# Moving the first batch's token loads and first products to later places in a two-layer kernel, and some consumers in its scans a step or two later

## The chip, the cores and the metric

The kernel is one program on one core of a Trainium2 chip. The core has five engines that each work through their own queue in order: TensorE (PE), VectorE (DVE), ScalarE (ACT), GpSimd (POOL) and SyncE (SP, which only issues transfers here; POOL issues transfers too). The metric is the device time of one execution in microseconds (us).

## The reference, cut to what matters

Eight batches of 512 tokens of 256 values go through two layers. In layer 0 a token-by-token recurrence runs over the 512 tokens (16 heads with 16x16 states), then each token goes through one of eight experts. Layer 1 is ordinary causal attention with 16 heads and a softmax, then a dense mixture of eight small experts.

```python
h = _layernorm(x) * (1 + ca) + sa
x = x + ga * _L0_attn_ref(h, ...)        # recurrence: M += beta * k (v - M k)
h = _layernorm(x) * (1 + cb) + sb
x = x + gb * _L0_ffn_ref(h, ...)         # top-1 of 8 experts, 256 -> 1024 -> 256
h = _layernorm(x) * (1 + ca) + sa
x = x + ga * _L1_attn_ref(h, ...)        # q, k, v products, softmax attention
h = _layernorm(x) * (1 + cb) + sb
x = x + gb * _L1_ffn_ref(h, ...)         # weighted sum over 8 dense experts
```

## The kernel before

All data is float32. The 512 tokens of every batch are cut into four token tiles of 128 (tile i = 0 to 3). For layer 0 all eight batches of one token tile are worked on together.

**The scans.** `scan(i)` is the recurrence over the 128 tokens of tile i, for all 128 pairs of batch and head at once. One step is four DVE instructions in a chain: L640 (state times key), L644 (sum), L650 (outer product), L655 (state minus update). While scan i runs, other work is queued between its steps: the preparation of tile i+1 (`front(i + 1)`) and the attention output, routing and part of the experts of tile i-1 (`follow(i - 1)`). Each such piece has a number, the scan step after which it is due. `run` calls the pieces in the order of these numbers, and `tc.issue_after(step)` holds a piece's instructions on DVE behind the DVE instruction that ends the step. Instructions on other engines get no such edge: their place follows from the order of the text and from when the tile scheduler, which fixes each engine's queue at build time, takes them to be ready.

**`front(i, at)`** works per pair of batches p and batch b = 2p + c. `stats(p)` loads tokens (SP) and makes mean and deviation on ACT (its last instruction is the square root, L501). `normal(p)` is two small DVE instructions (L517, L518). `turn(b)` normalizes and transposes (ACT L140 and L145, PE L143), `project(b)` makes the q, k, v and beta products (PE L535, L539; ACT L543 to L549). `squares(b)` sums q*q and k*k on DVE (L553). `roots` and `scales` (ACT L565, L566; DVE L570; POOL L588) follow for each half of the batches, and `heads` at `at + 46` and `at + 49` lays out K and V for the next scan. `at` is 30 for tile 1 and 47 for tiles 2 and 3.

**`attend(i)`**, in its end: `roots` (DVE L824, behind ACT L809), `rest(b)` adds the attention output to the tokens (ACT L828, POOL L831 and L832 for tiles 0 to 2, then a store), and `stats(b)` takes their statistics on DVE (L840, L841).

**The slot tiles.** `route(i)` sorts the 1024 tokens of a token tile by expert into 15 slot tiles of 128 rows and scatters them to `hs_d` (POOL L1023, eight indirect transfers). `experts(i)` then walks over the slot tiles j = 0 to 14. `turn(j)` loads the rows (SP L1061, tile `hslot`, two buffers) and transposes them (PE L1064, ACT L1068). The first half of a slot tile is 32 matmuls (L1083) with weights w0, the second half 16 matmuls (L1102) with weights w1. `fetch(j, part)` gathers an expert's weights, 1 MB for w0 and as much for w1 (POOL L1044, two buffers each). The result takes a bias on POOL (`ysb`, L1108) and is stored to `ys_d` (POOL L1109). The order in the text is: fetch (0,0), (0,1), (1,0), then for each j the first half, fetch (j+1, 1), rows of j+1, second half, bias and store, fetch (j+2, 0).

When all 15 slot tiles of a token tile are stored, each batch's 128 results are gathered back (POOL L1117), multiplied by a gate (POOL L1153) and added to the tokens in memory by an accumulating transfer (POOL L1154, `x<-yrow`). For token tile 2 the gathered tile is `yrow`, from a tag with two buffers.

**The last stretch of layer 0.** For the last token tile, `x_last` takes a buffer of that same tag `yrow`. It is loaded at the start of `experts(3)`, ahead of `turn(0)` on SP:

```python
if i == NT - 1:
    x_last = fp.tile([P, D], F32, tag="yrow", name="x_last", bufs=2)
    nc.sync.dma_start(x_last, x2d[0][i])
```

The loads of the first batch's other three token tiles (`xs_first`, SP L1113) stand in the text at j = 7. The beginning of layer 1 for the first batch (`prologue`, 14 pieces: `norm`, five staged pieces of normalizing, transposing and v products, `both(0)` and `both(1)` with the q and k products of three token tiles at L261, then the same for the last token tile) is merged into the list of `experts(3)`, whose halves stand at 10j and 10j + 3, by

```python
last.append((102 + 4 * k if k < NT + 4 else 201 + k, piece))
```

so that `both(0)` stands at 126 and `both(1)` at 130, between the halves of slot tiles 12 and 13. `place1` loads layer 1's expert weights (`ew`, SP L212, two transfers of 1 MB) just ahead of `experts(3)`. After the last slot tile comes the return of the first batch's last token tile (`rows`, POOL L1117, DVE L1128 and L1129 with `x_last`), then the last prologue pieces, and the first scores of layer 1 (PE L1304).

Of the kernel before, what the change touches and what calls it, by code (L numbers as in the profile page):

```python
# [11 lines left out]
F32 = mybir.dt.float32  # L12
# [7 lines left out]
P = 128  # L20
B = 8
S = 512
D = 256
# [40 lines left out]
def tile_two_layers(ctx: ExitStack, tc: tile.TileContext, t: dict, out: bass.AP):  # L64
# [217 lines left out]
    with ExitStack() as l0:  # L282
# [166 lines left out]
        def front(i, at):  # L449
# [102 lines left out]
            def squares(b):  # L552
                nc.vector.tensor_reduce(  # L553
                    ss[:, :, b, :], got["sq", b].rearrange("p s (n d) -> p s n d", d=HD),
                    AX.X, ALU.add,
                )
# [51 lines left out]
            for p in range(B // 2):  # L608
                if i > 0:
                    pieces.append((at + 8 * p, lambda p=p: stats(p)))  # L610
                    pieces.append((at + 8 * p + 4, lambda p=p: normal(p)))
                elif p == 0:
                    pieces.append((at, stats_first))
                for c in range(2):
                    b = 2 * p + c
                    pieces.append((at + 8 * p + 3 * c + 4, lambda b=b: turn(b)))

                    late = 4.5 if i == 0 else 0
                    pieces.append((at + 8 * p + 3 * c + 4 + late, lambda b=b: project(b)))
                    pieces.append((at + 8 * p + 3 * c + 11, lambda b=b: squares(b)))  # L620
            for h in range(B // n):
                last = at + 16 * h + (23 if i else 39)
                pieces.append((last, lambda h=h: roots(h)))
                pieces.append((last + 2, lambda h=h: scales(h)))
            pieces.append((at + 46, lambda: heads("K", qk[:, 1], 1.0)))
# [31 lines left out]
        def attend(i, qk, V, x1, norms):  # L657
# [198 lines left out]
            for h in range(2):  # L856
                pieces.append((16 * h + 25, lambda h=h: roots(h)))
                for b in range(4 * h, 4 * h + 4):
                    pieces.append((13 * h + 25 + b, lambda b=b: rest(b)))
                    pieces.append((12 * h + 29 + b, lambda b=b: stats(b)))  # L860
            return got, pieces


# [167 lines left out]
        def experts(i, slot, idx):  # L1031


            if i == NT - 1:
                x_last = fp.tile([P, D], F32, tag="yrow", name="x_last", bufs=2)
                nc.sync.dma_start(x_last, x2d[0][i])
            ws = {}

            def fetch(j, part):
                if j >= NSLOT:  # L1040
                    return
                first, n = (0, WONE) if part == 0 else (WONE, WROW - WONE)
                w = fp.tile([P, n], F32, tag=f"w{part}", name=f"w{part}_{i}_{j}", bufs=2)
                issued["fetch"] = nc.gpsimd.indirect_dma_start(  # L1044
                    out=w,
                    out_offset=None,
                    in_=t[f"wrows{part}"],
                    in_offset=bass.IndirectOffsetOnAxis(ap=idx[:, j : j + 1], axis=0),
                    bounds_check=NE * P - 1,
                    oob_is_err=False,  # L1050
                ).ins
                ws[j, part] = w

            turned = {}

            def turn(j):

                if j >= NSLOT:
                    return
                hr = fp.tile([P, D], F32, tag="hslot", name=f"hslot{i}_{j}", bufs=2)  # L1060
                issued["rows"] = nc.sync.dma_start(hr, hs_d[i][j * P : (j + 1) * P, :]).ins  # L1061
                pt = bank()
                for c in range(2):
                    nc.tensor.transpose(  # L1064
                        pt[:, c * P : (c + 1) * P], hr[:, c * P : (c + 1) * P], ident
                    )
                hT = fp.tile([P, 2, P], F32, tag="hTs", name=f"hTs{i}_{j}", bufs=2)
                nc.scalar.copy(hT, pt[:, :D].rearrange("p (c t) -> p c t", c=2))  # L1068
                turned[j] = hT

            for j, part in ((0, 0), (0, 1), (1, 0)):
                fetch(j, part)
            turn(0)
            for j in range(NSLOT):
                hT = turned.pop(j)
                act = fp.tile([P, NFC, P], F32, tag="act", name=f"act{i}_{j}")
                w = ws[j, 0]
                for half in range(2):
                    ph = bank()
                    for q in range(4):  # L1080
                        f = half * 4 + q
                        for k in range(2):
                            nc.tensor.matmul(  # L1083
                                ph[:, q * P : (q + 1) * P],
                                w[:, k * FF + f * P : k * FF + (f + 1) * P],
                                hT[:, k, :],
                                start=(k == 0),
                                stop=(k == 1),
                            )
                    for q in range(4):  # L1090
                        f = half * 4 + q
                        nc.scalar.activation(  # L1092
                            act[:, f, :], ph[:, q * P : (q + 1) * P], AF.Relu,
                            bias=w[:, 2 * FF + f : 2 * FF + f + 1],
                        )
                fetch(j + 1, 1)
                yield
                turn(j + 1)
                w = ws[j, 1]
                py = bank()  # L1100
                for f in range(NFC):
                    nc.tensor.matmul(  # L1102
                        py[:, :D], act[:, f, :], w[:, f * D : (f + 1) * D],
                        start=(f == 0), stop=(f == NFC - 1),
                    )
                ysb = fp.tile([P, D], F32, tag="ysb", name=f"ysb{i}_{j}", bufs=2)
                nc.scalar.copy(ysb, py[:, :D])
                nc.gpsimd.tensor_add(ysb, ysb, w[:, NFC * D :])  # L1108
                nc.gpsimd.dma_start(ys_d[i][j * P : (j + 1) * P, :], ysb)  # L1109
                fetch(j + 2, 0)  # L1110
                if i == NT - 1 and j == NSLOT // 2:
                    for k in range(i):
                        nc.sync.dma_start(w1["xs"][:, k, :], x2d[0][k])  # L1113
                yield

            def gather(b, dst):
                nc.gpsimd.indirect_dma_start(  # L1117
                    out=dst,
                    out_offset=None,
                    in_=ys_d[i],  # L1120
                    in_offset=bass.IndirectOffsetOnAxis(ap=slot[:, b : b + 1], axis=0),
                )

            if i == NT - 1:
                rows = [w1["rows"][:, b * D : (b + 1) * D] for b in range(B)]
                for b in range(B):
                    gather(b, rows[b])
                nc.vector.tensor_mul(rows[0], rows[0], gates[1][:, 0, :])  # L1128
                nc.vector.tensor_add(w1["xs"][:, i, :], rows[0], x_last)  # L1129
                yield  # L1130
                with tc.issue_after(w1["ready"]):
                    for b in range(1, B):
                        nc.vector.tensor_mul(rows[b], rows[b], gates[1][:, b, :])
                        nc.gpsimd.dma_start(x2d[b][i], rows[b], accum_op=ALU.add)
                yield
                return

            if i < NT - 2 and "fetched" not in w1:
                fetched = ap.tile([P, P, HD], F32, tag="K", name="fetched")
                w1["fetched"] = fetched.rearrange("p t d -> p (t d)")  # L1140
            queue = []
            for b in range(B + DEPTH[i]):
                if b < B:
                    if i < NT - 2:
                        yr = w1["fetched"][:, b * D : (b + 1) * D]
                    else:
                        yr = fp.tile([P, D], F32, tag="yrow", name=f"yrow{i}_{b}", bufs=2)
                    with tc.issue_after(issued["scatter" if i == NT - 2 else "fetch"]):
                        gather(b, yr)
                    queue.append(yr)  # L1150
                if b >= DEPTH[i]:
                    yr, k = queue.pop(0), b - DEPTH[i]
                    nc.gpsimd.tensor_mul(yr, yr, gates[1][:, k, :])  # L1153
                    nc.gpsimd.dma_start(x2d[k][i], yr, accum_op=ALU.add)  # L1154
                yield
# [123 lines left out]
        begun = list(prologue(0, first, w1["xs"], (tuple(range(NT - 1)), (NT - 1,))))  # L1279

        for k, piece in enumerate(begun):
            last.append((102 + 4 * k if k < NT + 4 else 201 + k, piece))
        run(last)

    rec.close()
# [345 lines left out]
```

## Time and profile before

| | us |
|---|---|
| median of 3 runs | 2255.97 (2253.57 to 2258.22) |
| the profiled execution's own time | 2256.92 |
| its span in the profile | 2255.2 |
| scans and what runs beside them, some 65 to 1107 | 1042 |
| attention of token tile 3, its routing, slot tiles of token tile 2 to the last, 1110 to 1211 | 101 |
| from the last matmul of token tile 2's slot tiles to the first of token tile 3's, 1211 to 1264 | 53 |
| the 15 slot tiles of token tile 3, 1264 to 1385 | 121 |
| return of the first batch's last tokens, to the first scores, 1385 to 1402 | 17 |
| layer 1, 1402 to 2255 | 853 |

The median is 0.95 us below the profiled execution's own time, and 1.7 us of that time lie around the span. Lines of the profile are read thus: a start in us from the beginning of the span, a duration in us, the engine, the line of the kernel (L1083 is line 1083), the operation, "out<-in" by the names of the program's tiles, shapes, and a count. What stands in brackets is how long the engine sat idle before and who ended that. "SPq" and "POOLq" are the queues that issue transfers.

### The profile page before, as it was taken

Reading aid. Unit: us, or ns where it says so; the run is one execution under the profiler, and the core shown is the slowest. Engines: PE = TensorE matmul, PEld = TensorE weight load, DVE = VectorE, ACT = ScalarE, POOL = GpSimd, SP = SyncE. Lnnn points to the kernel's source line nnn. Section 1 sums busy time; section 2 is a strip of 40 time slices with the busy share of each in tenths; the row PEclk is TensorE's granted clock in tenths of the full one; section 3 lists DMA queues with packets and bytes.
Section 4 is the critical chain, followed back from the end, with each engine's and each line's share of the span. In section 5 each row is a group of like instructions: output and inputs, shape, how many; then the busy total and the mean of one; then the engine's idle time right before and its main releaser. Section 6 shows DMA issues by size and latency. Waiting matters only on the chain.

```text
span 2255.2 us, 32318 instructions
## 1 busy us (share of the span) xinstructions
PE 1726.5 (77%) x10874; PEld 1195.3 (53%) x10874; DVE 1595.2 (71%) x4533; ACT 1076.8 (48%) x2672; POOL 589.8 (26%) x791
## 2 busy tenths in 40 slices
PE   5334027479696887939893597999999999999997
PEld 3212025359574785738762596565555555555553
DVE  3899999899987999899652002686675767666654
ACT  5144025465356643613341244877475665747431
POOL 1102014145253453624374443010201011010111
PEclk9566567599798998959996798899999999999998
DMA  5110000178002680138665582000101010100001
GB/s 161 48 45 10 0 1 11 34 263 312 32 13 86 251 309 31 46 143 300 178 112 172 178 315 61 13 12 12 23 14 22 15 29 11 24 12 13 17 17 17
DMA packets 88630, 189.57 MB, mean 84 GB/s; under 512 B 13689, under 2 KB 67105, under 8 KB 75665
## 3 DMA queue, kind: packets, MB, share of 16 engines
q0 software_dynamic: 33696, 137.43, 19.0%
q1 hardware_dynamic: 54768, 50.09, 7.9%
q8 instruction: 86, 1.41, 0.3%
q14 instruction: 80, 0.65, 0.1%
HBM read 175.10 MB, written 36.93 MB: 94 GB/s over the span
## 4 chain that ended last, share of the span: by engine, by line
PE 42%; DVE 26%; issue 14%; ACT 7%; DMA 6%; POOL 5%; SPq 0%; POOLq 0%; ACTq 0%; DVEq 0%
PE ps L1469 6%; DVE state L644 6%; PE ps L1083 5%; PE ps L1330 5%; DVE state L655 5%; DVE terms L640 5%; DVE upd L650 5%; PE ps L1102 4%; PE ps L1304 3%; PE ps L535 3%; PE ps L1351 2%; DMA w<-in_wrows,idx 2%; PE ps L261 2%; DVE sc L1313 1%; PE ps L244 1%
## 5 line engine op out<-in xcount | busy, mean ns | idle before, releaser
L1318 ACT ACTIVATE pr<-sc,low 128x384 f32<-128x384 f32 (+3 forms) x512 | 255.6, 556 | 196.7 <-DVE low L1313 194.5
L1313 DVE CUSTOM_DVE_ANT_0 sc<-ps,strips 128x384 f32<-128x384 f32 (+3 forms) x512 | 225.4, 485 | 87.4 <-PE ps L1304 56.6
L1083 PE MATMUL ps<-hTs,w 128*128 128x128 f32 x1920 | 236.8, 284 | 19.9 <-DMA w<-in_wrows,idx 13.5
L1083 PEld LDWEIGHTS ps<-hTs,w 128*128 128x128 f32 x1920 | 233.3, 200 | 27.2 <-issue 13.1
L644 DVE TENSOR_REDUCE state<-terms 128x16 f32<-128x272 f32 x512 | 227.2, 444 | 15.8
L655 DVE TENSOR_TENSOR state<-state,upd 128x256 f32<-128x256 f32 x511 | 223.1, 437 | 14.8
L1469 PE MATMUL ps<-ew,hTd 128*128 128x512 f32 x512 | 232.9, 608 | 0.0
L640 DVE TENSOR_TENSOR terms<-state,K 128x256 f32<-128x256 f32 x512 | 216.0, 422 | 14.4
L1102 PE MATMUL ps<-w,act 128*128 128x256 f32 x960 | 220.8, 384 | 6.1 <-DVE dm L820 6.1
L650 DVE TENSOR_TENSOR upd<-K,state 128x256 f32<-128x256 f32 x511 | 214.2, 419 | 15.6
L1092 ACT ACTIVATE act<-ps,w 128x128 f32<-128x128 f32 x480 | 137.1, 371 | 152.8 <-PE ps L1083 151.7
L1330 PE MATMUL ps<-cst,pr 128*128 128x128 f32 x1280 | 192.4, 296 | 14.9 <-DVE low L1313 12.5
L1102 PEld LDWEIGHTS ps<-w,act 128*128 128x128 f32 x960 | 180.0, 193 | 29.5 <-DVE dm L820 6.6
L1474 DVE SCALAR_TENSOR_TENSOR accd<-ps,wtd,accd 128x256 f32<-128x256 f32 x256 | 123.8, 483 | 99.8 <-PE ps L1469 87.7
L1330 PEld LDWEIGHTS ps<-cst,pr 128*128 128x128 f32 x1280 | 149.8, 149 | 83.7 <-DVE low L1313 24.2
L1469 PEld LDWEIGHTS ps<-ew,hTd 128*128 128x128 f32 x512 | 96.4, 193 | 121.2 <-issue 107.6
L1478 POOL TENSOR_TENSOR accd<-accd,bc_g 128x256 f32<-128x256 f32 x28 | 20.4, 728 | 528.5 <-DVE accd L1474 528.5
L1044 POOL DMA_INDIRECT w<-in_wrows,idx x120 | 123.2, 1027 | 127.8 <-ACT hTs L1068 55.9
L1304 PE MATMUL ps<-kT,qTc 32*128 32x128 f32 (+3 forms) x1024 | 132.2, 491 | 5.4 <-DVE low L1313 3.8
L1339 DVE COPY prT<-ps 128x512 f32<-128x512 f32 (+3 forms) x256 | 117.0, 484 | 10.4 <-PE ps L1330 10.0
L674 PE MATMUL ps<-cst,V 128*128 128x128 f32 x64 | 12.5, 378 | 124.2 <-DVE V L646 124.2
L1337 ACT COPY prT<-ps 128x512 f32<-128x512 f32 (+3 forms) x256 | 98.9, 414 | 8.6 <-PE ps L1330 8.2
(264 smaller groups left out, 2939.4 us busy)
## 6 DMA issues: line engine op xcount, KB each, us to landing
hs<-zero SPq DMA_DIRECT2D x4, 1920.0 KB
hslot<-hs SPq DMA_DIRECT2D x60, 128.0 KB
ys<-ysb POOLq DMA_DIRECT2D x60, 128.0 KB, 3.8
x<-in_x SPq DMA_DIRECT2D x32, 128.0 KB
strips<-strip_d SPq DMA_DIRECT2D x16, 256.0 KB
out<-accd POOLq DMA_DIRECT2D x32, 128.0 KB, 3.1
wm<-in_wmod SPq DMA_DIRECT2D x4, 768.0 KB
xt<-in_x SPq DMA_DIRECT2D x12, 256.0 KB
```

Source lines behind the costliest of these rows:

```text
L640: nc.vector.tensor_mul(term[:, :, :HD], M, K[:, s, :].unsqueeze(1).to_broadcast([P, HD, HD]))
L644: nc.vector.tensor_reduce(delta, term, AX.X, ALU.add)
L650: nc.vector.tensor_mul(upd, K[:, s, :].unsqueeze(2).to_broadcast([P, HD, HD]), delta.unsqueeze(1).to_broadcast([P, HD, HD]),)
L655: yield nc.vector.tensor_sub(M, M, upd).ins
L1083: nc.tensor.matmul(ph[:, q * P : (q + 1) * P], w[:, k * FF + f * P : k * FF + (f + 1) * P], hT[:, k, :], start=(k == 0), stop=(k == 1),)
L1092: nc.scalar.activation(act[:, f, :], ph[:, q * P : (q + 1) * P], AF.Relu, bias=w[:, 2 * FF + f : 2 * FF + f + 1],)
L1102: nc.tensor.matmul(py[:, :D], act[:, f, :], w[:, f * D : (f + 1) * D], start=(f == 0), stop=(f == NFC - 1),)
L1304: made = nc.tensor.matmul(pscs[r][:, :W], qT[rows, g, o, i * P : (i + 1) * P], kT[rows, g, :W], start=True, stop=True,)
L1313: nc.vector.tensor_tensor_reduce(out=sc[:, :W], in0=pscs[r][:, :W], in1=strips[:, n, S - W :], scale=1.0, scalar=3.0e38, op0=ALU.add, op1= ...
L1318: nc.scalar.activation(pr, sc[:, :W], AF.Exp, bias=low, scale=-1.0)
L1330: nc.tensor.transpose(pt[:, (i - j) * P : (i - j + 1) * P], prs[r, i][:, j * P : (j + 1) * P], ident,)
L1469: nc.tensor.matmul(pe, hT[0][:, k, cols], ew[:, k, e : e + 2, :], start=(k == 0), stop=(k == 1),)
```

## The change

In `front`, for token tiles 1 to 3: `normal` goes from `at + 8p + 4` to `at + 8p + 5`; `turn` and `project` go one step later, `squares`, `roots` and `scales` two steps later; `heads` stays. In `attend`, `stats` goes one step later for all token tiles. In `experts(3)`, the load of `x_last` leaves the start and stands with the three loads of `xs_first` at j = 7, all four held on SP behind the load of the ninth slot tile's rows. In the list of the last stretch, `both(0)` and `both(1)` of the first three token tiles go from 126 and 130 to 151 and 152, behind the second half of the last slot tile at 143. No instruction is added or removed.

```diff
@@ front
                 if i > 0:
                     pieces.append((at + 8 * p, lambda p=p: stats(p)))
-                    pieces.append((at + 8 * p + 4, lambda p=p: normal(p)))
+                    pieces.append((at + 8 * p + 5, lambda p=p: normal(p)))
                 elif p == 0:
                     pieces.append((at, stats_first))
                 for c in range(2):
                     b = 2 * p + c
-                    pieces.append((at + 8 * p + 3 * c + 4, lambda b=b: turn(b)))
-
-                    late = 4.5 if i == 0 else 0
+                    pieces.append((at + 8 * p + 3 * c + (5 if i else 4), lambda b=b: turn(b)))
+
+                    late = 4.5 if i == 0 else 1
                     pieces.append((at + 8 * p + 3 * c + 4 + late, lambda b=b: project(b)))
-                    pieces.append((at + 8 * p + 3 * c + 11, lambda b=b: squares(b)))
+                    pieces.append((at + 8 * p + 3 * c + (13 if i else 11), lambda b=b: squares(b)))
             for h in range(B // n):
-                last = at + 16 * h + (23 if i else 39)
+                last = at + 16 * h + (25 if i else 39)
@@ attend
-                    pieces.append((12 * h + 29 + b, lambda b=b: stats(b)))
+                    pieces.append((12 * h + 30 + b, lambda b=b: stats(b)))
@@ experts
-            if i == NT - 1:
-                x_last = fp.tile([P, D], F32, tag="yrow", name="x_last", bufs=2)
-                nc.sync.dma_start(x_last, x2d[0][i])
...
                 if i == NT - 1 and j == NSLOT // 2:
-                    for k in range(i):
-                        nc.sync.dma_start(w1["xs"][:, k, :], x2d[0][k])
+                    x_last = fp.tile([P, D], F32, tag="yrow", name="x_last", bufs=2)
+                    with tc.issue_after(issued["rows"]):
+                        nc.sync.dma_start(x_last, x2d[0][i])
+                        for k in range(i):
+                            nc.sync.dma_start(w1["xs"][:, k, :], x2d[0][k])
@@ the last stretch
         for k, piece in enumerate(begun):
-            last.append((102 + 4 * k if k < NT + 4 else 201 + k, piece))
+            place = 102 + 4 * k if k < NT + 2 else 145 + k if k < NT + 4 else 201 + k
+            last.append((place, piece))
```

## The prediction, made before the result was known

> **What bounds the kernel now.** I read the busy time by stage first, then the chain of waits through the last stretch of layer 0, then the queues of POOL and PE there, and last the waits of DVE during the scans. The stages (columns: window, length, busy us of PE, PEld, DVE, ACT, POOL, granted clock, DMA share, GB/s):
>
> ```profile
> 890.00:1110.00 220.00, 170.89 (x1281) 150.83 (x1279) 198.05 (x506) 85.62 (x266) 97.83 (x133) 0.88 0.49 165
> 1211.00:1264.00 53.00, 0.29 (x2) 0.00 (x0) 4.25 (x6) 0.37 (x1) 30.43 (x34) 0.55 0.64 186
> 1264.00:1385.00 121.00, 119.48 (x784) 109.53 (x784) 3.21 (x11) 51.64 (x166) 44.99 (x54) 0.98 0.60 217
> 1385.00:1402.00 17.00, 6.26 (x30) 5.30 (x34) 4.64 (x14) 4.08 (x12) 11.83 (x14) 0.60 0.33 78
> ```
>
> In the scans DVE is the pace (198 of 220). Then 53 us follow in which PE does nothing, then 121 in which PE is never idle, then a hole of 17. The chain of waits names the end of the 53:
>
> ```profile
> 1257.20 3.16 DMA x<-yrow
> 1260.49 0.34 SPq L1036
> 1260.87 3.10 DMA hslot<-hs
> 1264.10 0.67 PE ps L1064 x2
> ```
>
> L1036 is `x_last`. It needs a `yrow` buffer, and gets one when the seventh accumulating transfer of token tile 2 has landed. The rows of slot tile 0 (`hslot`) stand behind it on SP. SP's own waits give 42.2 us to L1036. The scatter that makes these rows had been over since about 1217, when `ew`, which also waits for it, was issued. So 42 us are an accident of a shared buffer tag. What would stop PE next, if the rows came early, is seen in POOL's timeline (start, duration, line, idle time before and who ended it):
>
> ```profile
> 1219.53 1.04 POOL L1044 DMA_INDIRECT w<-in_wrows,idx  x1 [0.30 <-issue]
> ...
> 1230.07 1.01 POOL L1044 DMA_INDIRECT w<-in_wrows,idx  x1 [0.30 <-issue]
> ...
> 1259.23 0.93 POOL L1154 DMA_DIRECT2D x<-yrow  x1 [0.30 <-POOL yrow L1153]
> 1271.75 1.09 POOL L1044 DMA_INDIRECT w<-in_wrows,idx  x1 [11.59 <-ACT hTs L1068]
> ```
>
> Four weight fetches are out by 1231: both halves of slot tiles 0 and 1. The fifth, tile 2's w0, is the next instruction on POOL after the last accumulate of token tile 2.
>
> **`x_last` and `xs_first`, behind the ninth rows.** SP issues `ew` at 1217.09 in 1.11 us, so `hslot` 0 can go out at 1218.2. It lands 3.1 us later as it did alone (1221.3), or at the latest when the traffic of `ew` ends: the DMA share stays at 0.8 or more until 1238. From landing to the first matmul took 1.1 us, and two slot tiles take 15.8 (1265.22 to 1281.05). So tiles 0 and 1 are done between 1238 and 1255, and PE then waits for tile 2's w0. POOL's queue is built before the run, and the change touches no line of POOL there, so I take the order of the trace: all eight gathers, then the fetch. It issues at 1259.23 + 0.93 + 0.30 = 1260.5 and lands 6.8 us later (median of the 22 fetches from 1270 to 1350): 1267.3. Before, tile 2 began at 1281.05. The clock is half again after that wait: the first half took 5.07 us after the 52.8 us hole against 3.73 in the next tile. With a cold tile's 8.58 us (1265.22 to 1273.80), tile 3 starts at 1275.8 instead of 1288.29: **12.5 us gained**. The other fetches keep up: tile 2's w1 issues at 1263.8 and lands at 1270.6, before its second half at 1272.4; tile 3's w0 lands at 1271.9. Ends of this term: 4.5, if the fetch takes the 14.8 us of the longest weight wait in the chain (at 1100.5), and some 36, if POOL's order lets fetches in between (a rival below).
>
> The four moved loads cost SP some 1.7 us (0.34 + 1.38) in the middle of tile 8, behind rows that are already out; the next rows are not needed for most of a tile, so nothing on the path. They add 0.5 MB to the transfers there. A fetch was issued at 1278.99 for a tile that began at 1288.29, 9.3 us later, and takes 6.8: 2.5 us of cover. The statistics and normalizing of these tokens, done at 1265 before, now fall into tiles 8 to 11 on a nearly idle DVE (3 of 121 us) and on ACT (52 of 121): nothing, or up to 1.2 us if two of ACT's 0.6 us pieces get ahead of a tile's activations.
>
> A rule speaks against splitting the tiles by a new hole. The Trainium skill, "TensorE: Matmul & The Clock Gate", section "Why this matters for your kernels", wants no PE gap over some 3 us, since one idle window brings half clock, and Part 1 puts the warming at about 3.4 us. By it a second cold start costs 1.7 us (half of 3.4, an estimate from that page), and the total would be 0.4 us smaller. The rows say 5.07 - 3.73 = 1.34, which the 12.5 contains.
>
> **`both(0)` and `both(1)`, behind the last slot tile.** PE was the pace (119.5 of 121), and these stood in its path:
>
> ```profile
> 1365.00 2.74 PE L261 MATMUL ps<-hTc,wqkv 128*128 128x384 f32 x8
> 1371.15 2.75 PE L261 MATMUL ps<-hTc,wqkv 128*128 128x384 f32 x8
> 1380.98 3.62 PE L1102 MATMUL ps<-w,act 128*128 128x256 f32 x16
> 1394.71 0.69 PE L179 MATMUL ps<-cst,xnc 128*128 128x128 f32 x2 [10.12 <-ACT xnc L172]
> ```
>
> The chain counts 2.58 us for each: 5.2 us leave the tile path. They enter a hole of 10.1 us that waits for bias, store and gather. Their ACT work (1.23 + 0.58, twice, some 1.4 us behind PE) ends about 7 us into the hole; ACT's next due instruction came at 1393.34, 8.8 us in. So **5.2 us gained**, with the hole's remaining 5 us as cover; without cover it would be 0. The clock had fallen by 1388, 3.4 us after the last matmul, and a hole of 4.9 still lets it fall: no gain there (if it held, up to 3 us, from 0.69 to 0.38 and the like).
>
> **The scans.** DVE's waits from 60 to 990:
>
> ```profile
> DVE stf L840 <- POOL x L832: 8.5, 8, 1.4
> DVE ss L553 <- ACT sq L549: 6.9, 5, 3.5
> DVE ms L824 <- ACT ms L809: 4.6, 3, 2.7
> DVE rsa L517 <- ACT sda L501: 3.8, 5, 0.9
> ```
>
> A step is 1.87 us (four instructions), and a wait of DVE moves everything behind it. `stats` (L840): the waits sit in scans 2 and 3, 0.94, 0.99, 1.40, 0.91 each. One step more between POOL and DVE can give one step at most, for POOL does one batch in about 2.6 us and stays the slower: **1.87 us in each of two scans, 3.7**. `squares` (L553): 2.53 and 3.49 are the first of scans 1 and 2, due exactly at their place (after 59 steps), so two steps (3.7 us) clear them. But counting L655 up to each line, `normal(1)` stands after 61 steps, and there ACT's deviation was ready only 0.2 and 0.04 us before DVE came. ACT got to this batch late because routing filled it until about 427 and 701, which the change does not shorten. So what `squares` stops waiting for, `normal(1)` waits for; and `normal(3)`, after 79 steps where its place allows 76, isn't held by its place at all. What is left is at most one step in each of scans 1 and 2, 1.2 us in scan 0 (0.33 + 0.86), 0.5 to 1 in small ones. I take **2.3** of 0 to 6. `turn`, `project`, `roots` and `scales` move nothing on the path: K and V are due 30 steps later. A loss is possible: the scans' gain of 6.0 lies between 9.7 (3.7 and 6) and a loss of 3.7 (both scans' chains on ACT late by the two steps, 7.4, against the 3.7).
>
> **The sum**: 12.5 + 5.2 + 6.0 = 23.7 off the profiled execution's 2256.9: **2233** (that execution is 1.0 us over the median).
>
> **Rivals.** *POOL lets expert work in between the gathers.* For: one fetch stands among them already (1230.07). Against: POOL is busy 30 of the 53 us and most of the rest is issue, and tile 0's bias and later fetches are behind the gathers in the text. PE would then go on from tile 1, at most 36 us earlier (tile 0 at about 1229 instead of 1265); halfway between 12.5 and 36 gives 24, and with the rest 35: 2222.
>
> *The rows stay late*, because something else of that list is put ahead of them on SP: only 5.2 and 6.0 are left, 2246. For: SP's order isn't the text's in full (`xs_first` stood before rows 2). Against: those loads are now held behind rows 8.
>
> *Slower: expert work gets ahead of `project(4)` on PE in scans 1 and 2.* Their places swap: 67 becomes 68, a tie with slot tile 0's first half. For: in an ordered queue PE would then wait for that tile's rows; the trace has such waits of 23.6 us (985 to 1205). Against: `project(4)` was ready at 464.52 and 736.49, the tile's matmuls at 471.01 and 743.41. Price: 10.4 us per scan by these rows (with the 3.84 of the half), up to 23.6; DVE pays in full, as it stands against ACT's deviation. It decides above 23.7/2 = 12 per scan; at 17 the end is 2267.
>
> **Chances.** The forecast 0.64 (its own ends: 2226 with the scans' 9.7 and the 3 us of a held clock, 2244 with the fetch's 4.5 and the scans' 3.7), interleaving 0.18, late rows 0.06, the swap at the price that makes it slower 0.07, and at a smaller price, which eats about what the end gains, 0.05. Faster by over 0.2% (4.5 us, about what a measurement here can tell from nothing): 0.64 + 0.18 + 0.06 = 0.88; within it 0.05; slower 0.07. The range 2216 to 2246 takes in the first three, and leaves out the swap and the far end of the interleaving, some 0.17.
>
> **What would show it.** Right: no L1036 wait on SP, rows 0 issued next to `ew`; the 52.8 us wait on L1064 falls under 25, and a new one of 12 to 28 us appears at tile 2's L1083, on its weights; the two L261 groups stand after the last L1102; L840's waits are about 2.2 per scan, L553's gone, L517's larger. Wrong: fetches among the gathers and no wait at tile 2 (then faster), or PE idle around `project(4)` (slower).

## The result, and the profile after

The change made no difference: 2253.81 us (median of 12 runs, 2246.41 to 2264.51) against 2253.86 (12 runs of the kernel before, 2248.09 to 2262.81). The ratio is 1.0005, with a 95% interval of 0.9988 to 1.0022, so between 2.7 us faster and 5.0 slower. 2233 was predicted.

The profiled execution of the changed kernel took 2264.51 us (span 2262.8), which is the slowest of its twelve. The long waits shown here come back in other kernels' traces below, but its total isn't the median's. Lines below its last stretch's edits have other numbers than before: L1061 is now the transpose of the rows, L1080 and L1099 are the first and second half of a slot tile, and L1305 the first scores.

The stages that answer to the first three of the four of before (same columns):

```profile
900.00:1120.00 220.00, 171.95 (x1304) 151.40 (x1292) 201.23 (x511) 87.77 (x271) 100.66 (x135) 0.89 0.49 166
1224.00:1248.00 24.00, 0.00 (x0) 0.00 (x0) 4.25 (x6) 0.37 (x1) 11.24 (x13) 0.61 0.82 292
1248.00:1395.00 147.00, 119.58 (x769) 111.13 (x770) 3.32 (x11) 47.48 (x159) 64.20 (x76) 0.89 0.59 198
```

The stretch in which PE does nothing is 24 us and no longer 53. But it begins at 1224 and not at 1211, so the scans and what lies behind them were some 13 us late, and the 15 slot tiles now take 147 us with 27 of them idle. PE's own waits in this stretch say where:

```profile
1248.17 0.66 PE L1061 MATMUL ps<-cst,hslot 128*128 128x128 f32 x2 [24.26 <-DMA hslot<-hs]
1281.83 6.31 PE L1080 MATMUL ps<-hTs,w 128*128 128x128 f32 x32 [16.05 <-DMA w<-in_wrows,idx]
1327.52 5.64 PE L1099 MATMUL ps<-w,act 128*128 128x256 f32 x16 [10.18 <-ACT act L1089]
1394.92 5.32 PE L261 MATMUL ps<-hTc,wqkv 128*128 128x384 f32 x16
1405.16 0.69 PE L179 MATMUL ps<-cst,xnc 128*128 128x128 f32 x2 [4.91 <-ACT xnc L172]
```

The first two and the last two are the ones that were predicted: rows early, then a wait for tile 2's weights, both products behind the tiles, a hole of 4.9. The third wasn't. In slot tile 6 PE waits for the activations, and what kept ACT is seen in its queue:

```profile
1313.63 0.37 ACT L1104 COPY ysb<-ps 128x256 f32<-128x256 f32 x1 [2.31 <-issue]
1326.92 0.30 ACT L126 ACTIVATE sdc<-mvc,cst 128x3 f32<-128x3 f32 x1 [12.92 <-DVE mvc L121]
1327.12 1.12 ACT L1089 ACTIVATE act<-ps,w 128x128 f32<-128x128 f32 x4
```

L126 is the square root of the first batch's statistics (`norm`). It stands ahead of tile 6's activations on ACT, and the loads of its tokens (`xs_first`) were issued only at 1311.57, behind the ninth rows. In the kernel before it ran in slot tile 0, after a wait that held PE up nowhere:

```profile
1267.01 0.30 ACT L126 ACTIVATE sdc<-mvc,cst 128x3 f32<-128x3 f32 x1 [1.84 <-DVE mvc L121]
```

Its place in the list is 102, in slot tile 10, but the scheduler put it four tiles earlier.

The second loss is in the scans. DVE's waits from 60 to 990, by the line that waits and the one that ends the wait (in all, times, longest):

```profile
DVE rsa L517 <- ACT sda L501: 29.6, 6, 13.2
DVE count L971 <- PE ps L966: 10.3, 2, 5.3
...
DVE stf L840 <- POOL x L832: 1.9, 2, 0.9
```

L553's 6.9 us are gone, and L840's 8.5 fell to 1.9. But L517 waits 29.6 where it waited 3.8: 13.15 at 473.44 in scan 1, 11.97 at 751.38 in scan 2.

```profile
473.44 0.17 DVE L517 RECIPROCAL rsa<-sda 128x2 f32<-128x2 f32 x1 [13.15 <-ACT sda L501]
```

ACT in scan 1, before and after (first fence before, second after):

```profile
461.10 0.46 ACT L496 ACTIVATE ps<-xt,mva 128x256 f32<-128x256 f32 x1
461.71 0.30 ACT L501 ACTIVATE sda<-mva,cst 128x2 f32<-128x2 f32 x1
...
470.58 0.38 ACT L1068 COPY hTs<-ps 128x256 f32<-128x256 f32 x1
```

```profile
455.90 0.20 ACT L494 ACTIVATE mva<-mva 128x2 f32<-128x2 f32 x1
467.19 0.37 ACT L1065 COPY hTs<-ps 128x256 f32<-128x256 f32 x1 [11.08 <-PE ps L1061]
467.46 0.48 ACT L496 ACTIVATE ps<-xt,mva 128x256 f32<-128x256 f32 x1
...
473.11 0.30 ACT L501 ACTIVATE sda<-mva,cst 128x2 f32<-128x2 f32 x1
```

The copy of slot tile 0's transposed rows (`hTs`) now stands between two instructions of `stats(2)`. PE cannot transpose those rows before they land (at 466.46, PE idle 11.46), so ACT waits 11.08 us for PE, `stats(2)` ends 11.4 later, and DVE, which had nothing else due, waits with it. By the end of scan 3 (the last L946) the changed kernel is at 983.98, the one before at 973.28.

### The profile page after: what moved, and what is told of

The parts are those of the page before. It is cut to its first block, busy times and chain, and to the rows that moved or that the text cites. A ratio compares the mean times of both kernels' runs of the same rounds, so it can differ in the third digit from the quotient of the medians.

```text
span 2262.8 us, 32307 instructions
## 1 busy us (share of the span) xinstructions
PE 1727.0 (76%) x10874; PEld 1196.3 (53%) x10874; DVE 1588.9 (70%) x4533; ACT 1078.0 (48%) x2674; POOL 591.4 (26%) x791
## 5 line engine op out<-in xcount | busy, mean ns | idle before, releaser
L1080 PE MATMUL ps<-hTs,w 128*128 128x128 f32 x1920 | 241.7, 287 | 34.1 <-DMA w<-in_wrows,idx 29.5
L1080 PEld LDWEIGHTS ps<-hTs,w 128*128 128x128 f32 x1920 | 238.0, 203 | 41.8 <-issue 29.9
L644 DVE TENSOR_REDUCE state<-terms 128x16 f32<-128x272 f32 x512 | 227.2, 444 | 15.6
L1099 PE MATMUL ps<-w,act 128*128 128x256 f32 x960 | 224.2, 387 | 10.8 <-ACT act L1089 10.8
L650 DVE TENSOR_TENSOR upd<-K,state 128x256 f32<-128x256 f32 x511 | 214.3, 419 | 15.7
L1089 ACT ACTIVATE act<-ps,w 128x128 f32<-128x128 f32 x480 | 137.6, 370 | 165.8 <-PE ps L1080 155.6
L1331 PE MATMUL ps<-cst,pr 128*128 128x128 f32 x1280 | 191.0, 294 | 15.1 <-DVE low L1314 12.2
L1099 PEld LDWEIGHTS ps<-w,act 128*128 128x128 f32 x960 | 182.0, 195 | 35.6 <-ACT act L1089 11.8
L1305 PE MATMUL ps<-kT,qTc 32*128 32x128 f32 (+3 forms) x1024 | 131.8, 490 | 4.7 <-DVE low L1314 2.8
L674 PE MATMUL ps<-cst,V 128*128 128x128 f32 x64 | 12.6, 377 | 117.4 <-DVE V L646 117.4
```

What stands on the lines that cost most here:

```text
L644: nc.vector.tensor_reduce(delta, term, AX.X, ALU.add)
L650: nc.vector.tensor_mul(upd, K[:, s, :].unsqueeze(2).to_broadcast([P, HD, HD]), delta.unsqueeze(1).to_broadcast([P, HD, HD]),)
L1080: nc.tensor.matmul(ph[:, q * P : (q + 1) * P], w[:, k * FF + f * P : k * FF + (f + 1) * P], hT[:, k, :], start=(k == 0), stop=(k == 1),)
L1089: nc.scalar.activation(act[:, f, :], ph[:, q * P : (q + 1) * P], AF.Relu, bias=w[:, 2 * FF + f : 2 * FF + f + 1],)
L1099: nc.tensor.matmul(py[:, :D], act[:, f, :], w[:, f * D : (f + 1) * D], start=(f == 0), stop=(f == NFC - 1),)
L1305: made = nc.tensor.matmul(pscs[r][:, :W], qT[rows, g, o, i * P : (i + 1) * P], kT[rows, g, :W], start=True, stop=True,)
```

## The experiments

Microseconds behind a ratio are (ratio - 1) times the median of the kernel before, 2251.5 to 2254.5.

### The parts

Four kernels hold one part each, or all but one. **front_only** is the kernel before with the lines of `front` from the change:

```diff
-  at + 8p + 4: normal(p)            +  at + 8p + 5
-  at + 8p + 3c + 4: turn, project   +  at + 8p + 3c + 5
-  at + 8p + 3c + 11: squares        +  at + 8p + 3c + 13
-  last = at + 16h + 23              +  last = at + 16h + 25     (roots; scales at last + 2)
```

> Only front's shifts (normal, turn and project a step later, squares, roots and scales two). New theory, from the trace of the changed kernel: in scans 1 and 2 the copy of slot tile 0's transposed rows (hTs) gets ahead of stats(2)'s second half (L496) on ACT, and ACT waits there for rows that land some 11 us later; DVE then waits 12 to 13 us for the third pair's deviation at L517 in each of the two scans, and saves the 2.5 and 3.5 at L553: slower than before by about 13 us (8 to 17). The prediction's step: faster by 2.3 (0 to 6), no L517 wait over 3 us.

Measured: 1.0084 (1.0061 to 1.0107), 18.9 us slower. L517 waits 12.85 and 12.01 in scans 1 and 2, and the last L946 comes at 985.31. The prediction's gain for this part is refuted, and the loss is somewhat above the new theory's 8 to 17.

**stats_only**:

```diff
-  12 * h + 29 + b: stats(b)         +  12 * h + 30 + b
```

> Only attend's stats one step later. The prediction's step: faster by 3.7, L840's waits 2.2 per scan. New theory, from the changed kernel's trace, where L840 keeps one wait of 0.93 in each of scans 2 and 3 out of 1.93 and 2.31: faster by 2.4. Rival: what L840 no longer waits for is waited for a line later, 0. All three are near what the comparison can tell; the waits decide.

Measured: 1.0002 (0.9987 to 1.0018). L840 keeps one wait of 0.93 in each of scans 2 and 3, as the new theory had it, but nothing is gained. L824's wait in scan 2 grew from 1.68 to 3.51, so the rival (waited for elsewhere) fits best.

**end_only** has the hunks of `experts` and of the last stretch, and no shift in the scans; **end_and_stats** has the shift of `stats` too.

```diff
-  x_last loaded at the start of experts(3)
+  x_last and xs_first loaded at j = 7, behind the ninth rows
-  both(0), both(1) at 126, 130
+  both(0), both(1) at 151, 152
```

> Only the two moves in the last stretch (x_last and xs_first behind the ninth rows; both(0), both(1) behind the last slot tile), the scans as before. The prediction's steps: faster by 17.7 (12.5 and 5.2). New theory, from the changed kernel's trace: the rows gain 9.5 up to slot tile 3, the statistics of the moved tokens stop ACT ahead of slot tile 6's activations and give back 12.1 (PE idle 10.2 and a half tile at half clock), both() gains 5.2: faster by 2.6. Rival: that stop is an accident of one execution, then faster by 14 to 18.

> The whole change without front's shifts. The prediction's steps: faster by 21.4 (12.5, 5.2, 3.7). New theory: no L517 wait over 3 us in scans 1 and 2, since front keeps its places; faster than before by about 5 (2.6 of the last stretch and 2.4 of stats), and so about 13 faster than the whole change. Rival (front's shifts do no harm): no more than 2 slower than the whole change.

Measured: 0.9955 (0.9937 to 0.9973), 10.1 us faster, and 0.9962 (0.9943 to 0.9981), 8.6 faster. Both traces show PE's wait in slot tile 6 (8.75 and 10.03), with L126 waiting 11.48 and 12.76 on ACT, so that stop isn't an accident of one execution. And L517 has no wait over 1 us in scans 1 and 2. The change without front's shifts is some 10 us faster than the whole. The new theory's 2.6 for end_only was too small by 7.5.

### The parts of the parts

**turn_only** is `normal`, `turn` and `project` a step later, **squares_only** is `squares`, `roots` and `scales` two steps later (the first two and the last two lines of front's diff above). **rows_only** and **both_only** are the two halves of end_only's diff.

> Of front's shifts only normal, turn and project a step later; squares, roots and scales stay. Theory: this is what puts the copy of slot tile 0's rows ahead of stats(2)'s second half on ACT, so the L517 waits of 12 to 13 in scans 1 and 2 are there in full, and the time is 14 to 19 slower than before (front's shifts as a whole: ratio 1.0084). Rival (it takes all of front's shifts): under 5 slower. The prediction gave this part 0.

Measured: 1.0067 (1.0050 to 1.0085), 15.1 us slower, L517 waits of 13.01 and 12.13. These three a step later are enough.

> Of front's shifts only squares, roots and scales two steps later. Theory: the order on ACT around stats(2) stays, no L517 wait over 3 us; the first L553 waits of scans 1 and 2 (2.5 and 3.5) are gone, and come back at L517 one batch later in part: faster than before by 0 to 6, 2.3 by the prediction's step. Rival (squares too moves the order): slower by 5 or more.

Measured: 0.9963 (0.9942 to 0.9984), 8.3 us faster, and no L517 wait over 1 us. The last L946 comes at 965.69, 7.6 before the kernel before. The first L553 waits (2.53, 3.49) are gone, but another one grew by almost as much: L971 (routing's count, from PE) waits 9.0 in all and not 3.4. So 7.6 had to come from elsewhere; the next section has it.

> Only the move of x_last and xs_first. The prediction's step: faster by 12.5. New theory: slot tile 3 begins 9.5 to 12 earlier, and the statistics' square root ahead of slot tile 6's activations on ACT takes 10 to 12 of it back: faster by 0 to 3. With the prediction's 5.2 for both() that would make 5 to 8 of the 10.1 (ratio 0.9955) that the two moves gained together.

Measured: 0.9978 (0.9962 to 0.9994), 5.0 us faster. PE's wait in slot tile 6 is 4.24 here, with L126 waiting 6.97.

> Only the move of both(0) and both(1) behind the last slot tile. The prediction's step: faster by 5.2, PE's hole before the last token tile's transposes 10.1 less 5.2 = 4.9. Rival 1 (a product too late for the hole delays the last transposes): under 3. Rival 2 (the clock holds through a hole of 4.9): 6 to 8.

Measured: 0.9953 (0.9935 to 0.9970), 10.6 us faster. In its trace PE's hole is 4.98, as predicted, and from slot tile 0's transpose to the first scores it takes 134.5 us, against 137.6 before (and 137.7 to 139.6 in five other kernels that leave this stretch as it was). That is a gain of 3 to 5. The granted clock fell in the shorter hole too (0.50 from 1386 to 1391), so the second rival isn't it. Layer 1 is 8.9 us shorter in this trace than in the one of before, but layer 1's time varies (last section); what the rest of 10.6 comes from isn't shown. The two halves together (10.1) are less than their sum (15.6), though by the intervals that could still be chance.

### The new waits taken away

**after_copy_held** is the whole change, with slot tile 0's copy held on ACT behind `stats(2)`:

```diff
+  if p == 2: issued["third", i] = (the square root L501 of stats(p)).ins
...
-  nc.scalar.copy(hT, ...)
+  if j == 0 and ("third", i + 2) in issued:
+      with tc.issue_after(issued["third", i + 2]):
+          nc.scalar.copy(hT, ...)
+  else:
+      nc.scalar.copy(hT, ...)
```

> The whole change, and in scans 1 and 2 the copy of slot tile 0's rows (hTs) is held on ACT behind the square root of stats(2) (L501). Theory (the copy ahead of stats(2) is what front's shifts cost): the L517 waits of 13.2 and 12.0 fall under 3 us, the end of scan 3 comes 9 to 13 us earlier than in the changed kernel, and the time is some 10 to 19 below the changed kernel's, 8 to 16 below the kernel before. Rival 1 (the price of front's shifts lies elsewhere, in squares or in later stages): no faster than the changed kernel. Rival 2 (the wait moves on: PE still takes slot tile 0's transpose ahead of batch 4's, so ACT or DVE waits a step later): under half of it gained.

Measured: 0.9941 (0.9921 to 0.9961), 13.3 us faster than before. ACT in scan 1, in the order of time (the lines are 4 to 6 further down in this kernel):

```profile
462.82 0.29 ACT L501 ACTIVATE sda<-mva,cst 128x2 f32<-128x2 f32 x1
469.64 0.37 ACT L1071 COPY hTs<-ps 128x256 f32<-128x256 f32 x1 [6.52 <-PE ps L1065]
```

The deviation is back at 462.82 (461.71 before). PE still waits 11.34 us for the same rows, ahead of batch 4's transpose. That isn't free: L517 now waits 4.37 and 4.41 us for the fourth pair (492.10 and 762.39), where under 3 was expected. But the last L946 of the scans comes at 972.32, 11.7 earlier than in the changed kernel. So it was in the main ACT's order and not PE's that DVE paid for.

**after_norm_held** is the whole change, with the square root L126 held behind the result's copy (L1104) of the last slot tile that the text has had by then:

```diff
+  issued["ysb"] = nc.scalar.copy(ysb, py[:, :D]).ins
...
   def norm(tiles):
+      (first batch, first three tiles) w1["behind"] = issued["ysb"]
...
+  with tc.issue_after(w1.pop("behind")):
       nc.scalar.activation(sd, mv[:, :, 1], AF.Sqrt, bias=ln_eps)
```

> The whole change, and the square root of the first batch's statistics (L126) is held on ACT behind the copy of a later slot tile's result, so that slot tile 6's activations do not stand behind it. Theory: PE's wait of 8.8 to 10.2 us in slot tile 6 and the half tile at half clock behind it (2.0) are gone, no wait takes their place; faster than the changed kernel by 10.5 to 12. Rival (what is late there comes back at slot tiles 10 and 11, where the five prologue pieces now stand close together): 0 to 5.

Measured: 0.9973 (0.9953 to 0.9993), 6.1 us faster than before, so some 7 faster than the whole change (1.0005). That is less than the 10.5 to 12 expected, though the intervals allow it. The square root runs at 1339.20 without a wait (its line is L128 there), and from tile 2's weights on PE has no wait over 0.6 in the slot tiles. **end_stats_norm** is end_and_stats with the same hold:

> The last run's whole change without front's shifts, with the same hold on the square root. Theory: on top of the 8.6 (ratio 0.9962) that the moves without front's shifts gained, the 8.8 to 10 us wait and the 2.0 to 2.8 of half clock in slot tile 6: faster than before by about 20 (0.991). Rival (as above): by 9 to 13.

Measured: 0.9910 (0.9890 to 0.9930), 20.3 us faster than before and some 12 faster than without the hold. **after_two_holds** is the whole change with both holds:

> The whole change with both holds (slot tile 0's copy behind stats(2); the square root of the moved statistics behind a later slot tile). Theory (these two waits are all that the change lost): 13.3 (0.9941) and the 7 to 12 of the second hold: faster than before by 20 to 25, ratio 0.990, which is about what the prediction gave the whole change (23.7). Rival: a further loss remains, not beyond 0.994.

Measured: 0.9916 (0.9887 to 0.9945), 18.9 us faster. The two queue places on ACT are what stood between the change and a gain near the predicted one. But its trace has the gain in other places than predicted: the last L946 of the scans comes at 972.22, only 1.1 earlier than before.

### A copy beside POOL's products

**scales_only** moves DVE's last three small instructions of `front` and POOL's products behind them, and leaves `squares` where it was:

```diff
-  pieces.append((last + 2, lambda h=h: scales(h)))
+  pieces.append((last + (4 if i else 2), lambda h=h: scales(h)))
```

> Of front's shifts only scales two steps later (DVE L570 to L572 and the POOL products L588 behind them); squares, roots, turn and normal stay. Theory, from the runs so far: what squares, roots and scales together gained (ratio 0.9963) is not L553's wait but one copy of the scan, L638, which took 3.7 us instead of 0.27 in scans 1 and 2 while POOL ran its L588 products back to back; with scales later POOL's products come after it: L638's 8.9 and 8.8 us in scans 1 and 2 fall to 5.5 or less, L553's waits of 2.5 and 3.5 stay, and the time is faster by 5 to 8. Rival (L553's wait is what counted): L638 as before or its loss moved to the next copy, faster by 0 to 2.

Measured: 0.9975 (0.9957 to 0.9993), 5.6 us faster, and the last L946 at 965.35, 7.9 earlier. L553's first waits stay (3.01 and 3.03). The copy L638 in scan 1, by line and shape (busy, mean ns, idle ahead of it), first in the kernel before, then in this one:

```profile
L638 DVE COPY terms<-V 128x128 f32<-128x128 f32 x17 | 8.9, 524 | 0.0
```

```profile
L638 DVE COPY terms<-V 128x128 f32<-128x128 f32 x17 | 5.1, 300 | 0.0
```

In scan 2 it is 8.8 and 5.0. So 7.6 us of the scans are in two copies. One of them, in the timeline of the kernel before with POOL beside it:

```profile
517.88 0.62 POOL L588 TENSOR_TENSOR v<-v,beta 128x256 f32<-128x256 f32 x1
518.42 3.68 DVE L638 COPY terms<-V 128x128 f32<-128x128 f32 x1
518.46 1.19 POOL L588 TENSOR_TENSOR qk<-qk,ss 128x256 f32<-128x256 f32 x2
...
521.93 0.61 POOL L588 TENSOR_TENSOR qk<-qk,ss 128x256 f32<-128x256 f32 x1
```

The same copy takes 0.27 us elsewhere. It counts as busy, so no list of waits shows it. `stats` a step later has the opposite effect: L638 takes 10.3 in scan 2 (8.8 before) and 5.2 in scan 3 (3.8). With L824's growth this takes back most of what L840 no longer waits for.

### Faster versions

**best** is end_stats_norm, with the last four gathers of token tile 2 moved into the list of the last stretch, at 4, 11, 14, 21 and 24 (the fifth is the last accumulate), and held on POOL behind the weight fetch that precedes them:

```diff
-  with tc.issue_after(issued["scatter" if i == NT - 2 else "fetch"]):
+  with tc.issue_after(issued["scatter" if i == NT - 2 and b < 4 else "fetch"]):
       gather(b, yr)
```

> As the one before, and the last four gathers of token tile 2 are held on POOL behind the fetch of slot tile 2's w0, so that this fetch stands after the fourth gather's iteration instead of the last. Theory (the fetch is late only because it stands behind the gathers on POOL): it issues as soon as slot tile 0's first half is over, some 12 to 20 us earlier, PE's wait of 15 to 16 at slot tile 2 falls under 5, and the time by 10 to 15 more: faster than before by 30 to 35. Rival (the transfers of gathers and weights share the queue, the gathers come late and x_last with them, or the fetches then fall behind by POOL's extra 4 us per gather in slot tiles 1 to 3): some of it comes back as weight waits at slot tiles 2 to 4, under 7 gained.

Measured: 0.9899 (0.9874 to 0.9924), 22.7 us faster than before, 2.4 more than end_stats_norm by the medians' ratio, which the intervals don't tell apart. That is the rival's case (under 7), and not the 30 to 35 of the theory. The fetch issued at 1246.23 (1259.53 in end_stats_norm), and the wait at slot tile 2 fell from 15.79 to 1.79. But ten small ones came behind it, 11.8 us in all. The first line is the wait at slot tile 2, the second the largest of the ten (L1086 and L1105 are the two halves):

```profile
1252.64 3.81 PE L1086 MATMUL ps<-hTs,w 128*128 128x128 f32 x32 [1.79 <-DMA w<-in_wrows,idx]
...
1268.99 5.23 PE L1105 MATMUL ps<-w,act 128*128 128x256 f32 x16 [2.29 <-DMA w<-in_wrows,idx]
```

From 1265 to 1330 a fetch takes 8.5 us here and 7.9 in end_stats_norm, against a slot tile's 7.25. That the transfers are now the pace isn't shown by this: the DMA share is 0.82 in this stretch, while end_stats_norm has 0.92 from 1275 to 1330 with PE busy for 54.9 of 55 us. POOL, which issues the fetches behind the moved gathers and the results' bias, is the rival, and no run separates the two.

**squares_end_norm** is end_stats_norm with squares_only's shift in the place of `stats`; **squares_end_norm_fetch** adds best's gathers to it.

> The two moves of the last stretch with the hold on the statistics' square root, and of the scans' shifts only squares, roots and scales (no normal, turn, project, no stats). Theory (the parts add): 8.4 (0.9963) and some 20 (0.991 for the last stretch with stats, which is worth 0): faster than before by 26 to 30, ratio 0.987. Rival (what the scans gain is lost in the tiles' transfers): as without squares, 0.991.

> As squares_end_norm, and the last four gathers of token tile 2 behind the fetch of slot tile 2's w0 on POOL. The first try of this gained 0 to 5 on top of the same kernel without it, since the wait of 15 us at slot tile 2 came back as ten waits of 0.4 to 2.3 on weights in slot tiles 2 to 9. Theory (the transfers are the bound there): within 4 of squares_end_norm. Rival: faster by 8 or more.

Measured: 0.9901 (0.9875 to 0.9926), 22.3 us faster than before, and 0.9883 (0.9850 to 0.9917), 26.4 faster. The second is the fastest kernel of the study by its median, and is faster than the kernel before and the changed one; its interval overlaps those of the next ones. Whether the squares add to the rest isn't settled: 0.9901 lies between the theory's 0.987 and the rival's 0.991, and nearer to the rival. Its slot tiles of token tile 2 begin 7.1 us earlier than end_stats_norm's (994.54 against 1001.62), and its token tile 3's only 1.7 (1230.21 against 1231.94).

## Why the prediction was wrong, step by step

**The rows (12.5).** The steps held one by one. `hslot` 0 landed between the two bounds; the fetch issued 1.22 us after the last accumulate's start (1274.27 to 1275.49; the prediction had 0.93 + 0.30), and landed 6.3 later; PE waited 16.05. Slot tile 3 began at 1291.65 against 1288.29, and the stretch began 12.6 later (its last matmul of token tile 2 ended at 1223.9 against 1211.3), so 9.3 were gained where 12.5 were predicted. The fetch issued 2.4 later behind the end of token tile 2's slot tiles than the prediction had it, and the cold tile took 9.82 us and not 8.58: its first half 6.31, so a cold start of 2.6 and not the 1.34 of the sum, nor the 1.7 estimated beside it. In the eight other traces with this move and the fetch in its old place, that first half takes 5.15 to 6.67, and the gain by the same measure is 9.2 to 13.7. So the term was about right, and the mechanism too.

**"Nothing, or up to 1.2 us" for the statistics of the moved tokens: this step failed.** It took them to fall into tiles 8 to 11, by the list's place 102, and weighed only their duration. Measured: 10.18 us of PE idle and 2.0 of half clock (5.64 against 3.62), in tile 6. The piece's place in the text doesn't hold an ACT instruction there, and what counts is not the 0.3 us that the square root takes but the 12.9 that it waits for a load which the same change had made late. The prediction had counted SP's queue and the transfers of the moved loads, not who waits for them in order on ACT.

**`both()` (5.2).** The hole and the products' place were right (10.12 to 4.98). In time both_only gained more than that (10.6, at least 6.8 by its interval), which stays unexplained.

**The scans (6.0): the step failed in size and in sign.** It took 2.3 of 0 to 6 for front's shift, with a loss of at most 3.7. (The forecast's slow end, 2244, even counts a gain of 3.7 in the scans; with that loss it is 2251, outside the range.) Measured: 18.9 slower. Two things were wrong. The loss bound counted a step or two of delay, and not a queue order that changes. The prediction had that as its slower rival, with the tie at 68 and a price of 10.4 per scan; measured were 9.4 per scan for front's shifts, 7.6 for `turn_only`. It was given 0.12 in all, because `project(4)` had been ready 6.5 us ahead of the tile's matmuls. But the queue's order is fixed at build time, and in the changed kernel the tile's matmuls did come first (at 467.62, ahead of batch 4's transpose). The rival's place was off too: it looked at PE and `project(4)`, while most of the wait that counts is ACT's, at the copy of slot tile 0's rows ahead of `stats(2)`. Why the scheduler puts the copy between `stats(2)`'s own instructions, though `stats(2)` is due at 63 in both kernels, the runs don't show.

**"`squares`: what it stops waiting for, `normal(1)` waits for."** Nearly right in kind: it came back, at L971 rather than L517. That `roots` and `scales` "move nothing on the path" was wrong: they moved POOL's products off a DVE copy, 7.6 us.

**`stats` (3.7).** L840's waits fell to one per scan, 0.93, lower than the 2.2 predicted; yet no gain can be told in the time, and in the trace L824 and L638 took most of it back.

The sum is near zero because losses in the scans and in slot tile 6 met the last stretch's gains (20.3 us faster with `stats` moved and neither loss, end_stats_norm). The parts don't add up to the whole, though: front_only, stats_only and end_only together make 9.3 us slower, and the whole measured 1.1 slower, at most 5.0. Where the difference lies is open, as the one profiled execution of the changed kernel is the slowest of its twelve. With both losses removed (after_two_holds) the change is worth 18.9 us of the 23.7 predicted. That the two come so close is in part luck: in that trace the first scores come 15.7 earlier than before, of which the scans give 1.1 (6.0 predicted), and layer 1, of which the prediction says nothing, is 8 shorter.

## What to carry to other kernels

When a change moves a load or a piece, look up every consumer of it on the in-order engines, and ask which instructions stand behind that consumer; price it by what it would wait for, not by how long it runs. Where two pieces come to stand at the same place, take the order to be open and give the swap a real chance, or hold the one that may not go first behind the other. And when a DVE instruction takes many times its usual time, read the busy rows too: no list of waits has it.

## What the runs showed of the hardware

A DVE copy of 128x128 f32 (L638, usually 0.27 us) took 3.68 and 4.14 us when it came in the midst of POOL's back-to-back products (L588, 0.6 us each), and ended 0.17 and 0.16 us after the start of the last of the seven products that came behind it (522.10 and 521.93 in the first case). The Trainium skill, "SBUF — State Buffer", section "Who interferes with whom", says that a DVE copy in a mode that uses both ports and a GpSimd instruction exclude each other, and that the one that starts first keeps the shared ports for that instruction. Taken for one instruction alone, this would cost the copy the rest of one product; the rows show that it was held until the last of the train had begun. Which mode L638 runs in, no row shows; both its ends lie in SBUF. The scan's four instructions were not slowed beside the same products (0.42 to 0.45 us each from 522.6 to 526 in squares_only); each of them reads only one tensor from SBUF, as this kernel keeps the state and the sums in PSUM.

Layer 1 takes a different time from trace to trace, with the same number of PE instructions (4728): from the first scores to the end 853.5 us in the kernel before and 837.9 in end_and_stats. The granted clock was 0.96 and 0.98, and PE was busy for 818.9 and 803.5 us, which is nearly the whole difference. These are two kernels, so whether a part of it is due to the change isn't shown. But the kernel before alone took 2239.87 to 2262.80 us in 90 executions, with a mean granted clock of 0.860 (in the longest) to 0.875, and on the whole the higher clocks go with the shorter times. So single executions differ by as much as the edits are worth.
